# One attention and FFN layer on one core: maxima, reads, loads and digits at other places of a period

## The chip, the cores and the metric

The kernel runs on one core of a Trainium2 chip. The metric is the device time of one execution in microseconds, lower is better. Three runs of the kernel before gave 1106.81, 1106.3 and 1104.47 us, median 1106.3.

## What is computed

The reference is one transformer layer on four sequences (B = 4) of 512 tokens and 1024 features: causal attention with 16 heads of 64 and rotary embedding, a LayerNorm over x plus attention, a linear layer with int8 weights and one scale per output row, and a second LayerNorm.

```python
q, k, v = x @ w_q.T, x @ w_k.T, x @ w_v.T          # split into 16 heads of 64
q, k = rope(q), rope(k)
scores = where(causal, q @ k.T, -1e9) / sqrt(64)
out = softmax(scores) @ v                          # back to (4, 512, 1024)
x = layernorm(x + out @ w_out.T)
x = layernorm(x + x @ (weight * scales[:, None]).T)
```

## The kernel before, in words

All large products run in fp32r, a format with fewer digits than float32. A float32 factor is therefore split into a high part and a low part ("digits"): `high_x` and `high_w` write the high part on ScalarE, `low_x` and `low_w` the low part on VectorE, and `diff_x`, `diff_w` a third tile d, which the product needs beside h and l. `split_w` is `low_w` followed by `diff_w`. `diff_x_apart` is `diff_x` in two instructions on GpSimd. The digits of a sequence's x live in `XD[b % 2]` (two sets), those of the weights of q, k, v in `WD[0..2]`. A product of one unit with one weight is 24 matmuls of 128x512: 16 with the h and l digits, alternating, then 8 with d.

A unit is one sequence and one pair of heads. There are 32 units: sequences 0 and 1 alternate over head pairs 0 to 7, then 2 and 3 alternate over head pairs 7 to 0. The loop over `u` makes one period for each unit. In period u TensorE runs, in this order: `attend(u-1)` (probabilities times values, L528), `scores(u)` (L420) and 72 "tickets" of the stream, which `take(n)` draws: the products k and v of unit u+1 and q of unit u+2 (L273). The last period draws the first four halves of the output projection instead (`out_product`, L200). After the loop come the rest of the output projection and the FFN (L200, L755).

The softmax of a unit goes in three groups g = 2, 1, 0 of the score rows, each in its own PSUM tile. For each group `maxima` takes a minimum with the mask (L444) and the row maxima (L447) on VectorE, `softmax` the exponentials on ScalarE (L461), and `transposes` a 32x32 block transpose on VectorE (L489) and a write to DRAM, `turned<-pr` (L490). `fetch(u, g)` reads it back in its transposed order, `prT<-turned` (L501: one DMA each for g = 2 and 1, two for g = 0). `attend(u)` needs all of them, at the end of the period. `shares` computes the reciprocals of the row sums and writes them (`turned_d`, L475), `fetch_shares` reads them back spread over the partitions (L481); `attended(u-1)` scales with them on GpSimd (L556, L558) and writes the result `ao` (L559). `turn_values` and `fetch_values` do for v what the transposes do for the probabilities (`turned_v`, L490, and `va`, L515).

A finished product is read out of PSUM by ScalarE (L293, after matmul 16) and VectorE (L321, after matmul 24). For q and k `swap` then copies even rows to odd rows and back with two DMAs (L245), and `rope` computes the rotary embedding, for q on GpSimd ("turned_q"), for k on VectorE ("turned_k"). PSUM has two buffers for the products (`pj`).

All DMAs of the loop are issued by SyncE (SP) in program order; an issue that must wait holds what is behind it. ScalarE, VectorE and GpSimd also run in the program's order. Work that must be done in some period, but not at a place that the loop itself names, is put on a plan with `later(u, slot, f)` and done at `run(u, slot)`. The slots stand in the loop in this order: "early", "turned_q", "between", "then", "after", "first", "turn", "mid", "second", "turned_k", "late", "end". Loads of x, of the weights and of `ao` go through three staging buffers (`stage`), which are used in turn; a load waits until the digits of what was there have been made.

Weights of the next head pair are loaded in every odd period that is followed by another head pair (`load_w`, three loads of 512 KB, L182). At four places the digits of x must be replaced: units 14 and 15 are the last of sequences 0 and 1, and units 30 and 31 the last of 2 and 3, after which `XD` receives the two halves of the output weight (L161). `new_sequence(u, b, begin)` does this: with `begin` it issues three loads at the first ticket of product v of unit u, that is in period u-1 inside `take(8)`; without, it makes the high digits and plans the rest. The first tiles of `ao` for the output projection are loaded by `load_ao(k)` (L187) during the products of the last unit, and their digits are put on the plan beside them.

## Time and profile before

The profiled execution took 1109.1 us and its span is 1106.9 us; the median of the runs shown is 1106.3 us. The mean granted TensorE clock is 0.969.

| what | from the profile |
|---|---|
| TensorE busy with matmuls | 1015.2 us, 92% of the span |
| VectorE, ScalarE, GpSimd busy | 774.4, 405.5, 258.8 us |
| DMA | 213.35 MB, mean 193 GB/s |
| the 32 periods and what is ahead of them | up to 824.8 us |
| the rest, output projection and FFN | 282 us |

A period is counted here from the copy of attend's result on ScalarE (L549) to the next one; the starts are read off the timeline of that line. Lengths in us by the period's number:

| period | 1 | 2 | 3 | 4 | 5 | 6 | 7 | 8 | 9 | 10 | 11 | 12 |
|---|---|---|---|---|---|---|---|---|---|---|---|---|
| us | 22.2 | 25.0 | 22.2 | 23.4 | 22.5 | 24.9 | 21.8 | 22.8 | 23.3 | 21.6 | 22.6 | 21.5 |

| period | 13 | 14 | 15 | 16 | 17 | 18 | 19 | 20 | 21 | 22 |
|---|---|---|---|---|---|---|---|---|---|---|
| us | 29.3 | 31.5 | 25.7 | 22.6 | 22.8 | 25.0 | 21.8 | 22.5 | 21.9 | 25.5 |

| period | 23 | 24 | 25 | 26 | 27 | 28 | 29 | 30 | 31 |
|---|---|---|---|---|---|---|---|---|---|
| us | 22.8 | 24.9 | 22.3 | 24.5 | 22.7 | 22.7 | 29.1 | 29.3 | 38.8 |

Period 0 and the start before it end at 65.5 us. In the profile's lines a tile's name stands as out<-in; "p" is a product, "s" the scores and attend's result, "pr" the probabilities, "sx", "sw" and "sa" the staged x, weights and ao, "raw" a product on its way to rope. Line numbers are those of the kernel before.

### The profile page before, as it was taken

The page shows a single profiled execution, that of the slowest core. Times are in us where ns is not written, and L with a number is a line of the kernel's source. Part 1 is how long each engine was busy: PE and PEld are TensorE (multiplying, and loading weights), DVE is VectorE, ACT ScalarE, POOL GpSimd, SP SyncE. Part 2 cuts the span into 40 slices and gives each one's busy share as a digit, 9 for nine tenths or more (in the row PEclk, how much of TensorE's full clock was granted, in tenths as well). Part 3 has the DMA queues.
Part 4 walks back from the last instruction along what each step waited for, and adds up shares of the span by engine and source line. Part 5 has one row for each costly group of instructions (what it writes and reads, how often), then busy time and mean ns, then how long its engine had stood idle before and what let it go on. Part 6 is the DMA issues. An engine that isn't in the chain of part 4 may idle for free.

```text
span 1106.9 us, 17050 instructions
## 1 busy us (share of the span) xinstructions
PE 1015.2 (92%) x6292; PEld 800.3 (72%) x6292; DVE 774.4 (70%) x1104; ACT 405.5 (37%) x873; POOL 258.8 (23%) x206
## 2 busy tenths in 40 slices
PE   9988999899999779899998999997689999999997
PEld 3667777777777657677776777775467888888885
DVE  5776676666767675766757666676678878787766
ACT  4434354343643344253542535434423121212010
POOL 0123342232422544233332334322010000000000
PEclk9989999999999889999999999998989999999999
DMA  7567667687687567676785766777843565656451
GB/s 270 148 190 235 217 195 235 189 251 221 193 257 230 164 217 232 194 221 210 220 256 167 235 205 194 241 227 218 248 141 106 155 156 135 165 126 160 100 129 57
DMA packets 286115, 213.35 MB, mean 193 GB/s; under 512 B 153264, under 2 KB 242352, under 8 KB 285904
## 3 DMA queue, kind: packets, MB, share of 16 engines
q1 hardware_dynamic: 282800, 201.91, 61.5%
q0 software_dynamic: 2224, 8.00, 1.9%
q10 hardware_dynamic: 1008, 2.36, 0.6%
q8 instruction: 50, 0.82, 0.3%
q14 instruction: 33, 0.27, 0.1%
HBM read 120.98 MB, written 74.45 MB: 177 GB/s over the span
## 4 chain that ended last, share of the span: by engine, by line
PE 45%; DMA 20%; DVE 17%; SPq 6%; issue 5%; ACT 5%; POOL 1%; DVEq 0%; ACTq 0%; POOLq 0%
PE y L200 13%; PE p L273 13%; PE f L755 11%; DMA prT<-turned 5%; PE s L528 5%; ACT pr L461 4%; DMA turned_v<-vt 3%; DVE nmx L447 3%; DMA raw<-raw 3%; DMA turned<-pr 2%; PE s L420 2%; DVE pr L489 2%; DVE w_d L224 2%; DVE s L444 2%; DVE raw L321 2%
## 5 line engine op out<-in xcount | busy, mean ns | idle before, releaser
L273 PE MATMUL p<-x_h,w_h 128*128 128x512 f32 x736 | 291.7, 396 | 3.7 <-DVE raw L321 3.7
L273 PE MATMUL p<-x_l,w_l 128*128 128x512 f32 x736 | 288.1, 392 | 0.0
L273 PE MATMUL p<-x_d,w_d 128*128 128x512 f32 x736 | 184.9, 393 | 17.4 <-DVE raw L321 9.4
L273 PEld LDWEIGHTS p<-x_d,w_d 128*128 128x128 f32 x736 | 137.0, 188 | 52.7 <-DVE raw L321 15.3
L461 ACT ACTIVATE pr<-s,nmx 128x512 f32<-128x512 f32 (+3 forms) x256 | 131.7, 526 | 93.0 <-DVE nmx L447 57.9
L273 PEld LDWEIGHTS p<-x_h,w_h 128*128 128x128 f32 x736 | 138.7, 188 | 34.9 <-DVE raw L321 4.5
L273 PEld LDWEIGHTS p<-x_l,w_l 128*128 128x128 f32 x736 | 138.9, 189 | 28.0
L556 POOL TENSOR_TENSOR ot<-ot,ot 128x448 f32<-128x448 f32 x32 | 36.8, 1150 | 436.7 <-ACT ot L550 436.7
L528 PE MATMUL s<-prT,va 64*64 64x64 f32 (+4 forms) x1408 | 96.0, 402 | 45.1 <-DMA prT<-turned 32.4
L489 DVE STREAM_TRANSPOSE pr<-pr 128x768 f32<-128x768 f32 (+1 forms) x96 | 102.1, 1064 | 40.7 <-ACT pr L461 39.0
L528 PEld LDWEIGHTS s<-prT,va 64*64 64x64 f32 x1408 | 72.1, 155 | 74.0 <-issue 60.8
L200 PE MATMUL y<-x_l,w_l 128*128 128x512 f32 x256 | 102.2, 399 | 7.9 <-DVE w_l L220 7.9
L447 DVE TENSOR_REDUCE nmx<-s 128x2 f32<-128x1024 f32 (+3 forms) x128 | 102.1, 820 | 9.1 <-PE s L429 6.1
L293 ACT ACTIVATE raw<-p 128x512 f32<-128x512 f32 x92 | 55.1, 599 | 142.2 <-PE p L273 140.9
L200 PE MATMUL y<-x_h,w_h 128*128 128x512 f32 x256 | 102.4, 400 | 2.4 <-DVE row L209 1.6
L321 DVE SCALAR_TENSOR_TENSOR raw<-p,raw 128x512 f32<-128x512 f32 x92 | 62.6, 680 | 52.9 <-PE p L273 37.1
L755 PE MATMUL f<-wf,x1hi 128*128 128x512 f32 x240 | 94.8, 395 | 2.0 <-ACT x1hi L728 2.0
L755 PE MATMUL f<-wf,x1lo 128*128 128x512 f32 x240 | 94.8, 395 | 0.3 <-DVE x1lo L729 0.3
L444 DVE TENSOR_TENSOR s<-s,bounds 128x256 f32<-128x256 f32 x116 | 48.9, 421 | 61.7 <-PE s L420 60.6
L420 PE MATMUL s<-qk 64*64 64x64 f32 (+5 forms) x1280 | 83.8, 368 | 1.6 <-ACT ot L550 1.6
L420 PEld LDWEIGHTS s<-qk 64*64 64x64 f32 x1280 | 65.6, 137 | 15.6 <-ACT ot L550 11.0
L549 ACT COPY ot<-s 128x512 f32<-128x512 f32 x32 | 18.7, 585 | 156.3 <-PE s L528 156.3
(120 smaller groups left out, 1357.0 us busy)
## 6 DMA issues: line engine op xcount, KB each, us to landing
turned<-pr SPq DMA_DIRECT2D x64, 384.0 KB, 2.7
raw<-raw SPq DMA_DIRECT2D x128, 128.0 KB, 4.1
turned<-pr SPq DMA_DIRECT2D x32, 512.0 KB, 2.9
prT<-turned SPq DMA_DIRECT2D x32, 512.0 KB, 4.3
prT<-turned SPq DMA_DIRECT2D x32, 384.0 KB, 4.2
turned_v<-vt SPq DMA_DIRECT2D x32, 256.0 KB, 4.6
va<-turned_v SPq DMA_DIRECT2D x128, 64.0 KB, 2.7
prT<-turned SPq DMA_DIRECT2D x32, 256.0 KB, 4.8
```

The lines of the kernel that those rows point to most:

```text
L200: nc.tensor.matmul(ps, lhsT=r[part][:, c, :], rhs=w[part][:, c, :], start=n in (0, 2 * NC), stop=n in (2 * NC - 1, NT - 1),)
L273: nc.tensor.matmul(ps, lhsT=w[part][:, c, :], rhs=r[part][:, c, :], start=n in (0, 2 * NC), stop=n in (2 * NC - 1, NT - 1),)
L293: nc.scalar.activation(raw_tile(u, k), ps, AF.Copy, scale=1.0 + X12)
L321: nc.vector.scalar_tensor_tensor(r, ps, -X12, r, op0=MUL, op1=ADD)
L420: nc.tensor.matmul(ps[c * D : (c + 1) * D, j, at + s0 : at + s1], lhsT=t[rows, 0, early : early + D], rhs=t[rows, 1, s0:s1], start=s0 == 0 ...
L444: nc.vector.tensor_tensor(diag, diag, tri, ALU.min)
L447: nc.vector.tensor_reduce(nmx[:, 2 * i : 2 * i + 2], ps[:, :, at : at + n], AX.X, ALU.max, negate=True)
L461: nc.scalar.activation(pr[:, :, at // P : at // P + i + 1, j, :].rearrange("p r k (c s) -> p r k c s", c=2), ps[:, j, at : at + n].rearran ...
L489: nc.vector.transpose(t.rearrange("p (r i s) -> p r i s", r=R, s=16) if by_place else t, by_place or t)
L528: nc.tensor.matmul(ps[j * D : (j + 1) * D, h, at : at + n], lhsT=lhsT, rhs=rhs, start=kb == 0 and at == h * D, stop=kb == NI - 1,)
L556: nc.gpsimd.tensor_tensor(o[:, D:], o[:, D:], o1[:, D:], ADD)
L755: nc.tensor.matmul(ps, lhsT=part[:, c, :], rhs=wfv[:, c, o], start=(c == 0 and part is hi), stop=(c == NC - 1 and part is lo),)
```

## The change

The diff has five parts. First, in the loop: all three `maxima` stand ahead of the transposes, and the three transposes follow each other. Second, on SP: the reads of groups 2 and 1 stand ahead of `take(8)`, in which the swap of k is issued, and the read of group 0 ahead of the write of the shares. "between" moves from ahead of `take(8)` to behind the reads of the shares, with a new slot "loads" behind it. Third, `new_sequence` is planned ahead for all four places: the loads of three staging buffers (two for unit 15) are issued in "early" of period u-1, the high digits are made in "second"; for unit 15 the third load goes to "loads" and its high digit to "end". Fourth, `diff_w(2)` of a new head pair goes from VectorE ("then") to GpSimd, in a new slot "beside" behind the rope of q. Fifth, for the last unit `load_ao(2)` goes to "loads", and the digits of `ao` tile 2 are made at the end of period 30 instead of in periods 30 and 31; `diff_w` of tile 0 follows its `low_w` at once; in period 0 `diff_x(0, 3)` goes from "late" to "between".

```diff
             if more and n == 0 and last:
-                load_ao(k)
+                if k < 2:
+                    load_ao(k)
+                else:
+                    later(u - 1, "loads", lambda: load_ao(2))
...
-            b_next = units[u + 2][0] if u + 2 < NU else B + b % 2
-            x_next = k == 2 and b_next != b
-            if x_next and n == 0:
-                new_sequence(u, b_next, True)
             if n == 2 * NC - 1:
                 nc.scalar.activation(raw_tile(u, k), ps, AF.Copy, scale=1.0 + X12)
-                if x_next:
-                    new_sequence(u, b_next, False)
                 if more and last:
-                    if k < 2:
-                        later(u - 1, ("after", "second")[k], lambda: high_w(k))
-                    else:
-                        high_w(k)
-                    l, d = (("turn", "mid"), ("late", "late"), ("after", "after"))[k]
-                    later(u - (k < 2), l, lambda: low_w(k))
-                    if k == 2:
-
-                        later(u, l, lambda: low_x(b_next, 0))
-                    later(u - (k < 2), d, lambda: diff_w(k))
+                    later(u - 1, ("after", "second", "end")[k], lambda: high_w(k))
+                    later(u - 1, ("turn", "late", "end")[k], lambda: split_w(k))
                 elif more:
...
                         later(u - 1, "end", lambda: low_w(2))
-                        later(u, "then", lambda: diff_w(2))
+                        later(u, "beside", lambda: diff_w(2, nc.gpsimd))
...
-        def new_sequence(u, b, begin):
-            if b == B + 1:
-                if begin:
-                    later(u - 1, "mid", lambda: load_x2(b, 0))
-            else:
-                for n in range(3):
-                    (load_x2 if begin else high_x)(b, n)
-            if begin:
-                return
+        def new_sequence(u, b):
...
+            first = (0, 1, 2) if u % 2 == 0 else (0, 1)
             if b <= B:
-                steps = (
-                    (u - 1, "late", each(low_x, 0)), (u - 1, "late", each(load_x2, 3)),
-                    (u - 1, "late", each(low_x, 1, 2)), (u, "between", each(high_x, 3)),
-                    (u, "between", each(low_x, 3)), (u, "between", each(diff_x, 0, 1)),
-                    (u, "late", each(diff_x, 2, 3)) if b == B else (u, "between", each(diff_x_apart, 2, 3)),
-                )
+                later(u - 1, "early", each(load_x2, *first))
+                later(u - 1, "second", each(high_x, *first))
+                later(u - 1, "late", each(low_x, 0))
+                later(u - 1, "late", each(load_x2, 3))
+                later(u - 1, "late", each(low_x, *first[1:]))
+                if u % 2:
+                    later(u - 1, "loads", each(load_x2, 2))
+                    later(u - 1, "end", each(high_x, 2))
+                    later(u, "between", each(low_x, 2))
+                later(u, "between", each(high_x, 3))
+                later(u, "between", each(low_x, 3))
+                later(u, "between", each(diff_x, 0, 1))
+                if b < B:
+                    later(u, "between", each(diff_x_apart, 2, 3))
+                else:
+                    later(u, "late", each(diff_x, 2, 3))
+                return
...
+        for u in range(1, NU):
+            b_next = units[u + 2][0] if u + 2 < NU else B + units[u][0] % 2
+            if b_next != units[u][0]:
+                new_sequence(u, b_next)
...
-            later(0, "late", lambda: diff_x(0, 3))
+            later(0, "between", lambda: diff_x(0, 3))
...
                 run(u, "turned_q")
+                run(u, "beside")
+                maxima(u, 0)
                 take(18)
-                transposes(u, 2)
-                maxima(u, 0)
                 softmax(u, 0)
-                transposes(u, 1)
-                transposes(u, 0)
+                for g in (2, 1, 0):
+                    transposes(u, g)
                 fetch(u, 2)
-                run(u, "between")
+                fetch(u, 1)
                 run(u, "then")
                 take(8)
+                fetch(u, 0)
                 shares(u)
-                fetch(u, 1)
-                fetch(u, 0)
                 fetch_shares(u)
+                run(u, "between")
+                run(u, "loads")
```

In the built program no instruction is added or dropped; 14 of VectorE's `diff_w` stand on GpSimd.

More of the change, by code (lines that the diff above doesn't have):

```diff
@@ L344, in new_sequence @@
             if b <= B:
-                steps = (
-                    (u - 1, "late", each(low_x, 0)), (u - 1, "late", each(load_x2, 3)),
-                    (u - 1, "late", each(low_x, 1, 2)), (u, "between", each(high_x, 3)),
-                    (u, "between", each(low_x, 3)), (u, "between", each(diff_x, 0, 1)),
-                    (u, "late", each(diff_x, 2, 3)) if b == B else (u, "between", each(diff_x_apart, 2, 3)),
-                )
-            else:
-                steps = (
-                    (u - 1, "late", each(load_x2, 1)), (u - 1, "late", each(high_x, 0)),
-                    (u - 1, "late", lambda: load_x2(b, 2, qkp.tile([P, 2, S], FP, tag="qk", name="last_2"))),
-                    (u, "early", lambda: load_x2(b, 3, qkp.tile([P, 2, S], FP, tag="qk", name="last_3"))),
-                    (u, "then", each(high_x, 1, 2)), (u, "after", each(low_x, 1, 2)),
-                    (u, "first", lambda: more_rows(2)), (u, "first", each(high_x, 3)),
-                    (u, "second", lambda: more_rows(3)), (u, "late", each(low_x, 3)),
-                    (u, "late", each(diff_x, 0, 1, 2, 3)),
-                )
@@ L362, in new_sequence @@
-            for step in steps:
+                later(u - 1, "early", each(load_x2, *first))
[7 more added lines that the diff above has]
+                    later(u, "between", each(low_x, 2))
@@ new lines, in new_sequence @@
+                later(u, "between", each(high_x, 3))
[6 more added lines that the diff above has]
+                return
+            for step in (
+                (u - 1, "mid", each(load_x2, 0)),
+                (u - 1, "late", each(load_x2, 1)), (u - 1, "late", each(high_x, 0)),
+                (u - 1, "late", lambda: load_x2(b, 2, qkp.tile([P, 2, S], FP, tag="qk", name="last_2"))),
+                (u, "early", lambda: load_x2(b, 3, qkp.tile([P, 2, S], FP, tag="qk", name="last_3"))),
+                (u, "then", each(low_x, 0)),
+                (u, "then", each(high_x, 1, 2)), (u, "after", each(low_x, 1, 2)),
+                (u, "first", lambda: more_rows(2)), (u, "first", each(high_x, 3)),
+                (u, "second", lambda: more_rows(3)), (u, "late", each(low_x, 3)),
+                (u, "late", each(diff_x, 0, 1, 2, 3)),
+            ):
```

## The prediction

> **What bounds the kernel now.** I read the page first: TensorE is busy 92% of the span, so an ordinary period cannot become much shorter. The shortest is 21.5 us (period 12). The other 30 together are (785.7 + 38.8 − 65.5) − 21.5 − 30 × 21.5 ≈ 93 us above it, 55 of them in periods 13 to 15 and 29 to 31. The waits say who holds TensorE:
>
> ```profile
> PE s L528 <- DMA prT<-turned: 32.4, 14, 5.3
> PEld p L273 <- DVE raw L321: 19.8, 16, 2.4
> SPq L515 <- DMA turned_v<-vt: 87.6, 19, 6.6
> ```
>
> (Engine, line, releaser: us in total, times, longest.) attend waits for the last prT read, the products wait for VectorE to empty a PSUM buffer, and SP itself waits for turned_v. The chain of waits through periods 13 and 14 (start, us, what) shows the dear places:
>
> ```profile
> 355.78 7.95 DMA prT<-turned
> ...
> 363.86 4.32 PE s L528 x29
> ...
> 380.68 3.12 DVE x_d L178 x2
> 383.80 0.60 DVE raw L321
> ...
> 388.97 6.34 DMA prT<-turned
> ```
>
> The loads of x stand ahead of the prT reads, the last of which lands 7.95 us after its issue (4.1 to 5.2 in periods 17 and 18), and in period 14 VectorE makes x digits before it empties k, so that swap and reads start 5 us late. Attend itself takes 4.3 us here, 2.4 in period 17: the clock has fallen. The same shows in stretches of period 18 (length, busy us of TensorE, its weight loads, VectorE, ScalarE, GpSimd, granted clock, DMA share, GB/s):
>
> ```profile
> 491.00:493.00 2.00, 0.98 (x9) 0.77 (x13) 2.00 (x3) 0.00 (x0) 0.00 (x0) 0.69 0.59 206
> 493.00:495.00 2.00, 2.00 (x22) 1.29 (x17) 1.93 (x2) 0.00 (x0) 0.00 (x0) 0.50 0.22 74
> ```
>
> A gap of 2.5 us costs the gap and some 2 us of half clock: even periods with gaps of 2.3 to 2.8 us last 24.5 to 25.5 us (period 4 alone 23.4), those with 1.6 to 1.8 us 22.5 to 22.8. Last, VectorE in odd period 17, which sets the product's wait:
>
> ```profile
> 452.97 1.25 DVE L489 STREAM_TRANSPOSE pr<-pr 128x1024 f32<-128x1024 f32 x1 [0.23 <-ACT pr L461]
> 454.14 0.87 DVE L444 TENSOR_TENSOR s<-s,bounds 128x256 f32<-128x256 f32 x2
> 455.04 1.02 DVE L447 TENSOR_REDUCE nmx<-s 128x2 f32<-128x256 f32 x2
> 455.98 0.97 DVE L489 STREAM_TRANSPOSE pr<-pr 128x768 f32<-128x768 f32 x1
> 457.85 0.98 DVE L489 STREAM_TRANSPOSE pr<-pr 128x768 f32<-128x768 f32 x1 [0.90 <-ACT pr L461]
> 458.75 1.18 DVE L224 TENSOR_TENSOR w_d<-w_h,w_l 128x1024 fp32r<-128x1024 f32 x1
> 459.86 0.68 DVE L321 SCALAR_TENSOR_TENSOR raw<-p,raw 128x512 f32<-128x512 f32 x1
> ```
>
> **Odd ordinary periods (12).** With the maxima ahead, group 0's are done at 452.7 + 0.87 + 1.02 ≈ 454.7 instead of 456.1; its exponentials (1.73 us) start behind the ScalarE read that ends at 454.7. The last transpose then ends at about 457.9 instead of 458.8, and without w_d (1.18) L321 ends at 458.6 instead of 460.5. The product's gap there (0.5 to 1.1 us, 1.13 in period 17) goes, and the last read is issued 1 us earlier. Against it: group 2's transpose is 1.7 us later, its write too; this is covered, since its read waited on SP until 459.3 for the third write's issue. The swap of k now waits behind the group 1 read, 384 KB or 1.5 us of a full queue (249 GB/s at 439 to 441 us), so k lands about 1 us later. Behind k on VectorE are turn_values and, in even periods, w_l (1.18), L321 of q (0.68), w_d (1.21) and w_l (1.22): they ended at 449.81, and period 17's first minimum started only then. So after an undisturbed even period the whole of this lateness, up to 1.6 us, passes to the odd period and eats its gain; after an even period with a lost clock there is room. Gain 1.1 us in about half, 0 to −0.3 in the rest: −0.4 each, −4.8. Bounds: −1.3 and +0.8 each.
>
> w_d takes 2.41 us on GpSimd (its row in period 16) and starts after the rope of q, at 456.1, so it ends at 458.5; the matmuls that read it start at 459.1 (40 matmuls of 0.225 us from 450.1). Cover 0.7 us; without it, TensorE waits for the difference. Beside GpSimd's two-step digits x_l takes 1.87 and 2.19 us (1.23 alone), but in period 16 L321 (0.69 at 438.80) ran unslowed beside this same w_d (438.19 to 440.60): I take 0; were each L321 slowed like x_l, 14 × 0.5 = 7 us. The Trainium skill, "SBUF — State Buffer", section "Who interferes with whom", says that a VectorE instruction with two SBUF inputs and a GpSimd one that reads SBUF lock each other out for the whole instruction. By it, VectorE's neighbours here (transposes with one input, L321 with one from PSUM) would not be touched, and the sum stays; a lock on all two-input instructions would make it up to 14 × 1.2 = 17 us worse.
>
> **Even ordinary periods (13).** The queue is full from the writes to attend (DMA share 0.9 to 1.07 between 481 and 489 us), so the order of reads matters little: only turned_d's 16 KB leave the path, about −0.3. But turned_d now lands behind the last read, some 2 to 2.5 us later, and SP holds the shares' reads, the three weight loads and turned_v behind it. In odd periods this moves 1.75 MB back; the loads' queue took 8.5 us to turned_v's landing, some of it at 102 GB/s, so part is made good. SP waits for that landing in the next even period before va, ao and the writes (5.4 us in period 18). I take +0.5 − 0.3 = +0.2 each, +2.6. Bounds: −0.8 (loads make it all good), +1.3 (all of it passes on).
>
> **The first replacement of x (13 to 15).** Period 13: the loads (1.5 MB, 3.9 us at 394 GB/s) move ahead of va, where the queue idles (0.2 to 0.5 DMA share at 449 to 453 in period 17), 5 us before the writes need it. va has 15 us of cover. The gap of 5.05 us goes and the half clock behind it: from 29.3 to an ordinary 22.2, −7. Period 14: L321 of k no longer waits for x_l and x_d (1.87 + 3.12), −5 of gap, −3 of clock, −1.7 at the products' x_h. A new wait: ScalarE makes the high digit of the third load at "end", ahead of the copy of attend's result; this load is issued on SP behind the shares, at about 20.4 us of the period, and lands some 4 to 5 us later (row<-in_x, the same size with little ahead of it: 3.9; sx: 5.8); its digit costs 1.06: the copy starts at about 26.5 instead of 22, and TensorE stands at the scores. Period 14 takes 26.5, −5. Period 15: without L321's late start −2.5, but x_d on GpSimd (1.88 + 3.23) ends late for the last products and the clock may fall: 24.2, −1.5. Sum −13.5; bounds −20 (all three at 22) and −7 (both new waits double).
>
> **The second (29 to 31).** Period 29 like 13: −7. Period 30 ends today in a chain that the change lengthens (start, us, what):
>
> ```profile
> 779.11 5.87 DMA sx<-in_wo
> ...
> 785.96 0.57 ACT ot L549
> ...
> 806.68 5.83 DMA row<-in_x
> ```
>
> Ahead of that load stands load_ao(2) now (512 KB, 1.3 us), and behind its digit ScalarE makes w_h and its scaled copy (1.04 + 1.06) before attend's copy; shorter gaps earlier in the period give back 2.6: +0.8. In period 31 the wait of 7.5 us for w_l (L200) goes, but the end hangs on row<-in_x, issued behind the shares, and these 1.0 us later behind turned_d; x_l and x_d follow on VectorE. +1.1. Sum −5.1; bounds −14 (the 7.5 us count, period 30 gains 1) and +1.
>
> **Period 0:** x_d's gap of 5.95 us goes, but the last prT read lands 0.6 us before that gap's end: −0.6, bounds −0.8 and +0.5.
>
> **Sum:** −4.8 + 2.6 − 13.5 − 5.1 − 0.6 = −21.4 us. The profiled span 1106.9 (execution 1109.1, 2.8 above the median) becomes 1085.5; from the median 1106.3: 1084.9, so 1085.
>
> On the clock: the Trainium skill, "TensorE: Matmul & The Clock Gate", section "What's actually happening", puts the fall after an idle window of about 3.4 us, so gaps of 2.5 us would cost nothing beyond themselves. Here they do, by the rows above (clock 0.69 and 0.50). By the page, six even periods would lie no lower and the slow rival below would be some 10 us cheaper.
>
> **Rivals.** (1) *Slower:* turned_d behind the last read. If all of its 2 to 2.5 us reaches turned_v, even periods start their writes 1.3 us later, the six with short gaps lose the clock as well (1.7 each), and the odd ones inherit VectorE's lateness (+0.8): 13 × 1.3 + 6 × 1.7 + 12 × 0.8 = +36.7, less 19.2 from the replacements and period 0, +17.5: 1124. It decides from 19.2 / 25 = 0.77 us lost per ordinary period. For it: turned_v already is SP's longest wait, 87.6 us. Against: the queue has slack at 467 to 469 us (share 0.71). 0.13. (2) *Better:* all odd periods gain 1.1, all even ones 0.3, and both new waits of ScalarE are covered (4.5 in period 14, 1.9 in 30 and 31): −13.2 − 3.9 − 18.6 − 6.4 − 0.6 = −42.7: 1064. For it: the waits named first do go; against: the full queue. 0.14. (3) *The loads come no earlier:* a staging buffer is free only after w_l at the period's begin (until 340.5 in period 13), then loads, va and the first write meet, and most of the gap reappears: replacements gain 5, ordinary periods 0: 1101. For it: the third buffer is the last one freed; against: the first write is needed 7 us later. 0.13. The forecast has 0.60.
>
> **How the numbers follow.** The measurement tells from no change what exceeds 0.2%, 2.2 us. The groups' low ends add up to −60.8, the high ends to +21.0; half the way from the sum to each gives 1065 to 1106, since they will not all fall on one side. That holds the forecast, rival 3 and half of 2, and leaves out rival 1: range 1065 to 1106. Faster: the forecast but for 0.02, rival 2 and 0.08 of rival 3: 0.80. Same: those 0.02 and 0.04 of rival 3: 0.06. Slower: rival 1 and the last 0.01 of 3: 0.14.
>
> **What would show it.** Right: prT reads of periods 13, 14, 29 land 4 to 5 us after issue; no L321 wait in odd periods; a wait of ScalarE's x_h on sx at the ends of periods 14 and 30. Wrong: even periods at 25 us throughout, SP's wait at L515 (now va) above 100 us, or VectorE's first minimum later than 2 us in odd periods. If period 13 stays above 24 us, the loads did not move.

## The result, and the profile after

The changed kernel takes 1143.4 us (median of 4 runs, 1140.1 to 1148.6), the kernel before beside it 1106.6 us: a ratio of 1.0334, 95% interval 1.0284 to 1.0384. The profiled execution took 1145.4 us, its span is 1143.6 us against 1106.9, its mean granted clock 0.950 against 0.969. The forecast was 1085 us, the range 1065 to 1106.

Where the 36.7 us of span went, in us, by the lengths of the periods (measured as in the table of before, from copy to copy on ScalarE; an ordinary period is one outside 0, 13 to 15 and 29 to 31):

| | before | after | difference | forecast |
|---|---|---|---|---|
| 12 odd ordinary periods | 268.8 | 267.9 | −0.9 | −4.8 |
| 13 even ordinary periods | 306.9 | 351.4 | **+44.5** | +2.6 |
| periods 13, 14, 15 | 29.3, 31.5, 25.7 | 22.3, 29.1, 25.9 | −9.2 | −13.5 |
| period 29 | 29.1 | 23.1 | −6.0 | −7 |
| period 30 | 29.3 | 40.3 | **+11.0** | +0.8 |
| period 31 | 38.8 | 39.5 | +0.7 | +1.1 |
| period 0 and the start | 65.5 | 64.5 | −1.0 | −0.6 |
| all behind the periods | 282.2 | 279.8 | −2.4 | 0 |

Two lines hold the whole loss. First the waits of TensorE and VectorE after (engine, line, releaser: us in total, times, longest); L523 is attend, L310 the read of a product's PSUM buffer, L237 the rope's first step:

```profile
DVE raw L237 <- DMA raw<-raw: 170.5, 31, 9.1
...
PE s L523 <- DMA prT<-turned: 70.8, 22, 5.9
...
PEld p L273 <- DVE raw L310: 3.8, 2, 1.9
```

The wait for VectorE is all but gone (it was 19.8), as forecast, but attend waits 70.8 us for the prT reads instead of 32.4, and VectorE 170.5 us for the swap of k instead of 72.1. SP's own waits say what they hang on (L476: the shares' reads, L510: va):

```profile
SPq L476 <- DMA turned_d<-rdenT: 128.4, 32, 5.5
SPq L510 <- DMA turned_v<-vt: 91.9, 28, 7.1
```

The first was 44.0 before:

```profile
SPq L481 <- DMA turned_d<-rdenT: 44.0, 30, 4.0
```

SP's issues around the begin of even period 8 (start, us, what) show how one wait becomes the other. Before, where the period begins at 227.5 us:

```profile
218.69 0.54 SPq L475 DMA_DIRECT2D turned_d<-rdenT  x1
219.33 1.50 SPq L501 DMA_DIRECT2D prT<-turned  x3
221.22 1.31 SPq L481 DMA_DIRECT2D share<-turned_d  x2
222.58 0.60 SPq L182 DMA_DIRECT2D sw<-in_wq  x1
...
224.23 0.59 SPq L490 DMA_DIRECT2D turned_v<-vt  x1
...
232.44 1.91 SPq L515 DMA_DIRECT2D va<-turned_v  x3
```

After, where it begins at 233.1 us:

```profile
224.47 1.29 SPq L496 DMA_DIRECT2D prT<-turned  x2
225.81 0.58 SPq L470 DMA_DIRECT2D turned_d<-rdenT  x1
230.59 1.31 SPq L476 DMA_DIRECT2D share<-turned_d  x2
231.95 0.60 SPq L182 DMA_DIRECT2D sw<-in_wq  x1
...
233.60 0.56 SPq L485 DMA_DIRECT2D turned_v<-vt  x1
```

And the chain of waits through the same stretch, after:

```profile
225.81 4.76 DMA turned_d<-rdenT
...
233.60 8.11 DMA turned_v<-vt
...
245.59 3.76 DMA turned<-pr
...
251.69 5.21 DMA prT<-turned
256.90 0.14 issue
257.03 4.32 PE s L523 x29
```

turned_d is 16 KB, yet it lands 4.76 us after its issue, just behind the last prT read. SP stands until then; the three weight loads and turned_v, which program order puts behind, are issued only from 231.95 on; turned_v stands behind 1.5 MB of weights and lands 8.6 us into the even period (233.60 + 8.11); only then does SP issue va (8.6 us into the period, 5.0 before), ao and the writes of this period's probabilities. Attend starts at 257.0, and TensorE has lost its clock meanwhile (length, busy us of TensorE, its weight loads, VectorE, ScalarE, GpSimd, granted clock, DMA share, GB/s):

```profile
253.00:255.00 2.00, 0.00 (x0) 0.00 (x0) 0.00 (x0) 0.00 (x0) 0.00 (x0) 1.00 1.12 309
255.00:257.00 2.00, 0.00 (x0) 0.00 (x0) 1.29 (x2) 0.00 (x0) 0.00 (x0) 0.64 0.18 41
257.00:259.00 2.00, 1.97 (x19) 1.14 (x22) 1.99 (x3) 0.00 (x0) 0.00 (x0) 0.50 0.05 16
```

Before, this period lasted 22.8 us with a gap of 1.8 us and full clock; now 28.5 with 5.2 and half clock. Over the 13 even periods the gaps ahead of attend grew from 25.2 to 55.7 us. The other 14 of the 44.5 us are slower work behind the gaps, most of it attend itself: it takes 52.4 us in these periods instead of 41.2, and over 3 us in 11 of the 13 instead of 6.

VectorE in odd period 17, beside the lines of before:

```profile
465.51 0.89 DVE L439 TENSOR_TENSOR s<-s,bounds 128x256 f32<-128x256 f32 x2
466.43 1.02 DVE L442 TENSOR_REDUCE nmx<-s 128x2 f32<-128x256 f32 x2
467.37 2.95 DVE L484 STREAM_TRANSPOSE pr<-pr 128x1024 f32<-128x1024 f32 x3
470.25 0.65 DVE L310 SCALAR_TENSOR_TENSOR raw<-p,raw 128x512 f32<-128x512 f32 x1
```

Maxima, three transposes, k's buffer: the order is the one wanted. It begins late here, because VectorE was still behind from the even period. On the mean of the odd ordinary periods L310 of k ends 10.2 us into the period (11.9 before), but the first minimum starts at 1.7 (1.0) and k's swap lands at 18.0 (15.8).

Last, the replacements. ScalarE's waits for the late loads, periods 14 and 30:

```profile
ACT x_h L165 <- DMA sx<-in_wo: 20.9, 1, 20.9
...
ACT x_h L165 <- DMA sx<-in_xT: 10.5, 1, 10.5
```

and the chain through the end of period 30 and into 31:

```profile
810.09 11.19 DMA sx<-in_wo
...
821.30 1.06 ACT x_h L165
822.36 0.95 ACT w_h L215
...
824.30 0.57 ACT ot L544
...
846.62 5.74 DMA row<-in_x
```

The load of 512 KB takes 11.2 us, with two loads of 512 KB from ScalarE's queue (the tables' rows) and ao's third tile issued 0.8 to 2.2 us ahead of it; two digits follow, and attend's copy comes 40.3 us into the period. In period 31 the wait for w_l is 3.3 us instead of 7.5, but TensorE waits 13.6 us for the row load behind the shares: the predicted exchange.

### The profile page after: what moved, and what is told of

Read it like the earlier page. It is cut to its first block, busy times and chain, and to the rows that moved or that the text cites. A ratio compares the mean times of both kernels' runs of the same rounds, so it can differ in the third digit from the quotient of the medians.

```text
span 1143.6 us, 17116 instructions
## 1 busy us (share of the span) xinstructions
PE 1022.3 (89%) x6292; PEld 807.8 (71%) x6292; DVE 766.5 (67%) x1090; ACT 401.1 (35%) x873; POOL 309.3 (27%) x220
## 4 chain that ended last, share of the span: by engine, by line
PE 42%; DMA 32%; SPq 9%; DVE 9%; issue 4%; ACT 3%; POOL 1%; DVEq 0%; ACTq 0%; POOLq 0%
PE y L200 13%; PE f L751 10%; PE p L273 9%; DMA turned<-pr 8%; DMA prT<-turned 7%; DMA turned_v<-vt 7%; PE s L523 6%; DMA turned_d<-rdenT 4%; PE s L415 3%; DMA raw<-raw 2%; SPq L245 2%; DVE pr L484 2%; SPq L496 2%; SPq L510 2%; ACT pr L456 1%
## 5 line engine op out<-in xcount | busy, mean ns | idle before, releaser
L523 PE MATMUL s<-prT,va 64*64 64x64 f32 (+4 forms) x1408 | 105.7, 434 | 72.0 <-DMA prT<-turned 70.8
L273 PEld LDWEIGHTS p<-x_d,w_d 128*128 128x128 f32 x736 | 137.5, 188 | 37.5 <-DVE raw L310 3.8
L523 PEld LDWEIGHTS s<-prT,va 64*64 64x64 f32 x1408 | 76.2, 166 | 105.7 <-issue 61.7
L551 POOL TENSOR_TENSOR ot<-ot,ot 128x448 f32<-128x448 f32 x32 | 39.4, 1231 | 411.7 <-ACT ot L545 399.0
L237 DVE TENSOR_TENSOR raw<-raw,sin_sb 128x512 f32<-128x512 f32 x33 | 23.4, 708 | 170.5 <-DMA raw<-raw 170.5
L200 PE MATMUL y<-x_h,w_h 128*128 128x512 f32 x256 | 102.6, 401 | 13.6 <-DVE row L209 13.6
L484 DVE STREAM_TRANSPOSE pr<-pr 128x768 f32<-128x768 f32 (+1 forms) x96 | 97.8, 1046 | 11.9 <-ACT pr L456 11.6
L310 DVE SCALAR_TENSOR_TENSOR raw<-p,raw 128x512 f32<-128x512 f32 x92 | 61.6, 670 | 59.5 <-PE p L273 59.3
L415 PE MATMUL s<-qk 64*64 64x64 f32 (+5 forms) x1280 | 86.9, 380 | 12.6 <-ACT ot L545 12.6
L415 PEld LDWEIGHTS s<-qk 64*64 64x64 f32 x1280 | 69.6, 143 | 25.5 <-ACT ot L545 21.3
```

The source lines that it names most:

```text
L200: nc.tensor.matmul(ps, lhsT=r[part][:, c, :], rhs=w[part][:, c, :], start=n in (0, 2 * NC), stop=n in (2 * NC - 1, NT - 1),)
L237: engine.tensor_tensor(rot, rot, sin_sb[:, k, :], MUL)
L273: nc.tensor.matmul(ps, lhsT=w[part][:, c, :], rhs=r[part][:, c, :], start=n in (0, 2 * NC), stop=n in (2 * NC - 1, NT - 1),)
L310: nc.vector.scalar_tensor_tensor(r, ps, -X12, r, op0=MUL, op1=ADD)
L415: nc.tensor.matmul(ps[c * D : (c + 1) * D, j, at + s0 : at + s1], lhsT=t[rows, 0, early : early + D], rhs=t[rows, 1, s0:s1], start=s0 == 0 ...
L484: nc.vector.transpose(t.rearrange("p (r i s) -> p r i s", r=R, s=16) if by_place else t, by_place or t)
```

## The experiments

All lengths below are us by class of period from each kernel's own profile; the time is the median, with the ratio to the kernel before on the same chip (its medians there: 1100.8 to 1102.7). "d" is the place of the shares' write turned_d on SP, "k" that of k's swap.

| kernel | odd | even | 13–15 | 29 | 30 | 31 | time | ratio (95%) |
|---|---|---|---|---|---|---|---|---|
| before | 268.8 | 306.9 | 86.5 | 29.1 | 29.3 | 38.8 | 1106.6 | |
| after | 267.9 | 351.4 | 77.2 | 23.1 | 40.3 | 39.5 | 1143.4 | 1.033 (1.028–1.038) |
| e1 | 258.5 | 340.3 | 77.1 | 21.7 | 37.6 | 39.7 | 1122.0 | 1.019 (1.014–1.024) |
| e2 | 258.1 | 307.8 | 73.2 | 22.2 | 34.9 | 37.7 | 1080.9 | 0.980 (0.975–0.986) |
| e3 | 266.3 | 353.6 | 85.0 | 25.9 | 37.9 | 41.3 | 1160.5 | 1.053 (1.048–1.058) |
| e4 | 260.3 | 353.2 | 79.9 | 22.8 | 35.2 | 39.0 | 1133.5 | 1.030 (1.025–1.036) |
| e5 | 269.7 | 301.4 | 72.7 | 23.8 | 32.1 | 34.9 | 1079.9 | 0.981 (0.978–0.984) |
| e6 | 254.7 | 347.5 | 78.8 | 22.5 | 37.0 | 39.9 | 1125.8 | 1.022 (1.019–1.025) |
| e7 | 255.8 | 303.7 | 73.1 | 22.4 | 28.8 | 37.5 | 1072.5 | 0.975 (0.971–0.979) |
| e8 | 252.6 | 280.1 | 71.2 | 21.3 | 31.0 | 37.0 | 1040.5 | 0.945 (0.942–0.948) |
| e9 | 259.5 | 297.7 | 85.0 | 28.2 | 28.3 | 35.5 | 1088.9 | 0.989 (0.985–0.993) |
| e10 | 263.4 | 312.4 | 86.0 | 27.2 | 28.8 | 36.9 | 1104.3 | 1.003 (1.000–1.006) |
| e11 | 268.4 | 308.0 | 71.9 | 22.5 | 28.6 | 38.6 | 1083.8 | 0.986 (0.983–0.990) |
| e12 | 275.7 | 300.6 | 80.1 | 21.6 | 38.0 | 40.2 | 1107.2 | 1.006 (1.004–1.009) |
| e13 | 256.4 | 293.2 | 80.2 | 22.6 | 36.1 | 38.5 | 1076.7 | 0.978 (0.974–0.982) |
| e14 | 275.2 | 281.7 | 72.3 | 24.0 | 31.2 | 34.9 | 1065.7 | 0.969 (0.965–0.973) |
| e15 | 266.7 | 279.0 | 87.1 | 27.8 | 28.5 | 37.8 | 1074.8 | 0.975 (0.972–0.979) |
| e16 | 257.2 | 278.1 | 72.2 | 23.3 | 28.5 | 36.5 | 1042.1 | 0.946 (0.943–0.950) |

The lengths are of one execution of each kernel. How far two executions differ can be seen where the programs are the same up to period 29: the odd and even periods together are 565.9 us in e2 and 559.5 in e7, 619.2 in the changed kernel and 613.5 in e4. Differences of 6 us, or of 8 in one class, therefore show nothing by themselves.

### The order of SP's reads: e1, e2, e3

e1 is the changed kernel with the write of the shares ahead of the last read:

```diff
                 take(8)
-                fetch(u, 0)
                 shares(u)
+                fetch(u, 0)
                 fetch_shares(u)
```

> The changed kernel with one step put back: the write of the shares (turned_d) and the two steps before it on VectorE stand ahead of the read of group 0 again; the read of group 1 stays ahead of the swap of k. Theory A (turned_d lands behind the last prT read and holds back the shares' reads, the weight loads, turned_v and so the writes of the next even period): the even ordinary periods fall from 27.0 us on the mean to 23.6 or less, their sum from 351 to about 307, SP's wait for turned_d from 128 to about 45 us in all, and the total to about 1143 - 44 = 1099 us (1090 to 1108). Rival B (k's swap behind the read of group 1 is what makes the even periods late): nothing of this, the evens stay at 26 to 27 us and the total above 1130. Rival C (the digit on GpSimd or the maxima): the same as B.

e2 puts back the whole order of reads:

```diff
                 fetch(u, 2)
-                fetch(u, 1)
                 run(u, "then")
                 take(8)
-                fetch(u, 0)
                 shares(u)
+                fetch(u, 1)
+                fetch(u, 0)
```

> The changed kernel with the whole order of SP's reads as before: only group 2 ahead of the eighth products and the swap of k, then the write of the shares, then groups 1 and 0. Theory A: as with the write of the shares alone put back, within some 5 us (1093 to 1105): the read of group 1 has no large part. Rival B: only this one falls, to 1100 or less, and the kernel with the write alone put back does not. Rival C: even periods stay at 26 to 27 us, the total above 1130.

e3 is the kernel before with this one part of the change (the same diff the other way, "between" where it was):

> The kernel before with only the order of SP's reads changed: groups 2 and 1 ahead of the eighth products, group 0 ahead of the write of the shares. Theory A: the even ordinary periods grow by about 3 us each, the total is about 1106 + 44 = 1150 us (1140 to 1165, since the odd periods have no gain to set against it here). Rival C (digit on GpSimd, maxima): the total stays at 1104 to 1110.

The order of reads is the whole loss of the ordinary periods: without it (e2) the changed kernel is 20 us faster than before, alone (e3) it costs 59 us. But e1 missed: one read less ahead of turned_d took only 11 us off the evens, not 44. By its profile turned_d still lands 17.6 us into the odd periods (15.8 in e2, 19.5 after), turned_v 6.9 us into the even ones (5.2, 7.9). That only e2 falls below 1100 us is what rival B had said, and e2 is faster than theory A allowed. Theory A could still stand in a wider form, that any read ahead of turned_d delays it. e1 differs from e2 in both: the read of group 1 stands ahead of turned_d and ahead of k's swap. Hence the next two.

### The write of the shares or the swap of k: e5, e6

e5: d right behind the read of group 2, k behind the read of group 1.

```diff
                 fetch(u, 2)
+                shares(u)
                 fetch(u, 1)
                 run(u, "then")
                 take(8)
                 fetch(u, 0)
-                shares(u)
```

> The changed kernel with the shares' write (turned_d) right behind the read of group 2, ahead of the read of group 1, which stays ahead of the swap of k. Theory A, by now in the form that whatever read stands ahead of turned_d's write on SP's queue delays it, and with it turned_v and the even periods (write behind one read: 26.2 us per even period, behind two: 27.0, behind group 2's alone: 23.7): turned_d lands at about 12 to 15 us of the odd periods, the evens fall to about 23.7 us, the total to 1080 to 1092 us (before 1101 to 1107). Rival B (the swap of k behind the read of group 1 sets the evens): the evens stay near 26 us, the total near 1120.

e6: k ahead, d still last.

```diff
                 fetch(u, 2)
-                fetch(u, 1)
                 run(u, "then")
                 take(8)
+                fetch(u, 1)
                 fetch(u, 0)
                 shares(u)
```

> The changed kernel with the swap of k ahead of the read of group 1 as before, but the shares' write (turned_d) still last, behind the reads of groups 1 and 0. Theory A: the evens stay at 26 to 27.5 us, the total at 1125 to 1150. Rival B: the evens fall to 23.7 us and the total to 1080 to 1095 us.

Theory A holds at both: e5 at 1079.9, e6 at 1125.8, with 23.2 and 26.7 us to the even period. SP's waits in e6, beside the changed kernel's 128.4 and 91.9:

```profile
SPq L476 <- DMA turned_d<-rdenT: 130.4, 32, 5.5
SPq L510 <- DMA turned_v<-vt: 106.4, 28, 7.3
```

The swap of k is not free: e5's odd periods are 11.6 us longer than e2's, since k lands 1.2 us later in the even ones and VectorE's first minimum in the odd ones starts at 2.2 instead of 1.2 us. Its even periods are 6.4 us shorter, so that its time is e2's.

### The weight loads between the shares and turned_v: e8, e12, e15, and e13, e14

One edit: SP issues the loads of a new head pair behind the write of turned_v.

```diff
                 run(u, "loads")
-                if u % 2 and u + 2 < NU - 1 and units[u + 2][1] != units[u + 3][1]:
-                    for k in range(3):
-                        load_w(k, units[u + 3][1])
...
                 if u + 1 < NU:
                     turn_values(u + 1)
+                if u % 2 and u + 2 < NU - 1 and units[u + 2][1] != units[u + 3][1]:
+                    for k in range(3):
+                        load_w(k, units[u + 3][1])
```

e8 has it on top of e7 (below), e12 on the changed kernel, e15 on the kernel before.

> The kernel with the old order of reads and the old last unit, and with the three weight loads of a new head pair (1.5 MB) moved on SP from behind the shares' reads to behind the write of turned_v. Theory A's last link (turned_v lands some 8 us after its issue because the weight loads stand ahead of it, and SP holds the even period's va reads and writes until then): turned_v lands 2 to 5 us after its issue in odd periods, SP's wait for it in even periods goes from about 5 us to under 1, their first write of probabilities from about 9 to about 7 us, and the 13 even periods fall from 23.7 to about 22 us: some 20 us less than its neighbour, about 1057 us. Rival F (the even periods are set by the bytes in the queue, not by when turned_v lands: the loads only move into the next period and delay its reads as much): the time stays within 5 us of the neighbour's.

> The changed kernel, its order of reads and all, with only the three weight loads of a new head pair moved from behind the shares' reads to behind the write of turned_v. Theory A's last link (the late write of the shares costs the even periods only because turned_v stands behind 1.5 MB of weights): turned_v lands about 3 us after its issue, 2 us or less into the even periods, these fall from 27.0 to 22 or 23 us, and the total to 1075 to 1095 us: the place of the shares' write costs next to nothing here. Rival I (the lateness of k's swap and of the shares themselves is enough): the total stays above 1115.

> The kernel before with one edit that the change does not have: the three weight loads of a new head pair behind the write of turned_v. Theory A (turned_v behind the weight loads sets the even periods whatever the rest does): the even periods fall from 307 to about 284 us, the odd ones from 269 to about 266, the total by 24 to 30 us, ratio about 0.975. Rival (it pays only together with the earlier maxima and loads): less than 10 us.

SP's issues in e8 around the begin of even period 8 (213.5 us):

```profile
204.45 0.56 SPq L472 DMA_DIRECT2D turned_d<-rdenT  x1
205.09 1.60 SPq L498 DMA_DIRECT2D prT<-turned  x3
208.20 1.32 SPq L478 DMA_DIRECT2D share<-turned_d  x2
210.68 0.34 SPq L487 DMA_DIRECT2D turned_v<-vt  x1
211.07 0.43 SPq L182 DMA_DIRECT2D sw<-in_wq  x1
...
214.34 3.45 SPq L512 DMA_DIRECT2D va<-turned_v  x4
```

va is issued 0.8 us into the period instead of 8.6 in the changed kernel; SP's wait for turned_v is 7.2 us in the whole run. The evens fall to 280 us, e8 to **0.945 of the time before**, the fastest of all: 32 us below e7, where theory A said 20. e15 shows that this needs nothing of the change: 26 us from the kernel before alone. e12 fell between its two theories: it takes back 43 us of odd and even periods, but 43.6 more than e8 remain, so the order of reads still costs something. e13 is e12 with k ahead (e6 and this edit), e14 with d ahead (e5 and this edit).

> The swap of k ahead of the read of group 1 as before, the write of the shares still behind the last read, the weight loads behind turned_v's write. Beside the changed kernel with the weight loads moved alone (1107 us, odd and even ordinary periods together 576 us) this differs by the place of k's swap. Theory K (what remained there is k's swap: VectorE begins its odd periods 2.7 us late): odd and even together fall to 533 to 545 us, the total to 1060 to 1075. Theory S (the shares' write still holds turned_v): they stay above 565 us, the total above 1090.

> The mirror of it: the write of the shares right behind the read of group 2, the swap of k behind the read of group 1, the weight loads behind turned_v's write. With the loads at their old place this took 1080 us, odd and even ordinary periods together 571. Theory K: these stay at 560 us or more, the total at 1065 to 1080. Theory S: they fall to 533 to 545 us, the total to 1040 to 1055.

Neither theory alone. Odd and even ordinary periods together:

| | loads ahead of turned_v | loads behind it |
|---|---|---|
| old order | 565.9 (e2) | 532.7 (e8) |
| k behind the read of group 1 | 571.0 (e5) | 556.9 (e14) |
| d behind the last read | 602.2 (e6) | 549.6 (e13) |
| both, as in the change | 619.2 (after) | 576.3 (e12) |

With the loads in the way d costs 36 us and k 5 (no more than two executions differ by), together 53; with the loads out of the way 17 and 24, together 44. What is left of d's price goes the same way: turned_v lands 2.4 us into the even periods of e13 and 0.7 us ahead of them in e8, and their first write is issued at 8.5 instead of 7.2 us. The late k costs the odd periods: VectorE around the end of even period 6 in e14 (197.4 us):

```profile
193.13 0.69 DVE L237 TENSOR_TENSOR raw<-raw,sin_sb 128x512 f32<-128x512 f32 x1 [4.38 <-DMA raw<-raw]
...
196.80 0.68 DVE L310 SCALAR_TENSOR_TENSOR raw<-p,raw 128x512 f32<-128x512 f32 x1
197.40 1.21 DVE L224 TENSOR_TENSOR w_d<-w_h,w_l 128x1024 fp32r<-128x1024 f32 x1
198.53 2.19 DVE L220 SCALAR_TENSOR_TENSOR w_l<-w_h,sw 128x1024 fp32r<-128x1024 f32 x1
```

VectorE waits 4.38 us for the swap, and what stands behind runs 3.3 us into the odd period; on the mean the first minimum starts at 2.8 us there, at 0.9 in e8.

### One part alone: e9, e10, e11, e16

e9 is the kernel before with the first part of the change (maxima ahead, transposes together), e10 with the fourth (v's third digit to GpSimd), e11 with the third (the loads of a new sequence). e16 is e8 with v's third digit back on VectorE.

```diff
-                take(18)
-                transposes(u, 2)
                 maxima(u, 0)
+                take(18)
                 softmax(u, 0)
-                transposes(u, 1)
-                transposes(u, 0)
+                for g in (2, 1, 0):
+                    transposes(u, g)
```

> The kernel before with one part alone: group 0's maxima ahead of the 18 products, the three transposes together behind its exponentials. Theory G (this part and the third digit on GpSimd share the gain of the odd periods, by how much earlier each lets VectorE empty k's buffer: 0.9 of 2.1 us): the 12 odd periods lose 4 to 5 us of their 269, the even ones nothing, the ratio is about 0.996. Theory H (the product's gap of 0.5 to 1.1 us is closed by either part alone): 8 to 10 us, ratio about 0.992. Rival: group 2's write, 1.7 us later, costs as much: ratio 1.000 or more.

```diff
-                        later(u, "then", lambda: diff_w(2))
+                        later(u, "beside", lambda: diff_w(2, nc.gpsimd))
...
                 run(u, "turned_q")
+                run(u, "beside")
```

> The kernel before with one part alone: the third digit of v's weights made by GpSimd behind the rope of q instead of by VectorE ahead of its read of k's buffer. Theory G: 5 to 7 us in the odd periods, ratio about 0.994. Theory H: 8 to 10 us, ratio about 0.992. Rival (GpSimd slows VectorE beside it, 7 to 17 us by the bounds of the prediction): ratio 1.000 or more, and the VectorE reads of PSUM beside the digit take over 0.69 us.

> The kernel before with one part alone: the loads of a new sequence at the begin of a period and their digits at their new places (the third digit of period 0 and the slot of the late digits with them); maxima, order of reads, v's third digit and the last unit as before. If the gain of the replacements comes from this part alone: periods 13 to 15 together fall from 86.5 to about 74 us, period 29 from 29.1 to about 22.5, the ordinary periods stay (odd 269, even 307), the total falls by 18 to 22 us, ratio about 0.982. Rival (they gain only because k's buffer is emptied earlier by the other parts): less than half of that.

e16, the fourth part undone in e8:

```diff
-                        later(u, "beside", lambda: diff_w(2, nc.gpsimd))
+                        later(u, "then", lambda: diff_w(2))
```

> The fastest version so far (old order of reads, old last unit, weight loads behind turned_v; 1040.5 us) with v's third digit back on VectorE ahead of its read of k's buffer. If the digit on GpSimd pays once turned_v no longer sets the pair of periods: the odd periods grow by 0.5 to 1.1 us each, the total to 1047 to 1053 us. If it pays nothing (alone in the kernel before it made 1.0028 of the time): within 3 us of 1040.5.

e9's ratio of 0.989 (0.985 to 0.993) fits theory H; in its profile the odd periods gain 9.3 us and the even ones, which no theory had named, 9.1. e10 closes the same gap (TensorE's wait for L321 falls from 19.8 to 4.3 us in both) and gains nothing in its time, against both theories. The rival's number came true (1.003), but not its reason: no VectorE read of PSUM beside GpSimd took over 0.69 us. In its profile the odd periods are 5.4 us shorter and the even ones 5.5 longer, differences that show nothing by themselves; SP's wait for turned_v is not shorter:

```profile
SPq L515 <- DMA turned_v<-vt: 93.1, 18, 7.2
```

(87.6 before.) The difference is what reaches SP. On the mean of the odd periods the maxima let group 0's write go 1.0 us earlier and the first read 0.6, turned_d lands at 15.5 instead of 16.1 us and turned_v is issued at 18.5 instead of 19.2. With the digit the first read is where it was (10.7, before 10.6); turned_d is issued 0.7 us earlier and yet lands at 16.5, and turned_v is issued at 19.6. So nothing that SP stops for comes earlier; why turned_d takes longer to land there was not tried. In e16 VectorE makes the digit again, and the time is e8's within its uncertainty: TensorE's wait for VectorE's read is 1.9 us in both, since the maxima close the gap by themselves (e9). e11 gives the replacements what was forecast for them: 13 to 15 lose 14.6 us, 29 loses 6.6, the ordinary periods nothing.

### The end of the units: e4, e7

The weights of the last unit as before, on the changed kernel (e4) and on e2 (e7):

```diff
-                if k < 2:
-                    load_ao(k)
-                else:
-                    later(u - 1, "loads", lambda: load_ao(2))
+                load_ao(k)
...
-                    later(u - 1, ("after", "second", "end")[k], lambda: high_w(k))
-                    later(u - 1, ("turn", "late", "end")[k], lambda: split_w(k))
+                    if k < 2:
+                        later(u - 1, ("after", "second")[k], lambda: high_w(k))
+                    else:
+                        high_w(k)
+                    l, d = (("turn", "mid"), ("late", "late"), ("after", "after"))[k]
+                    later(u - (k < 2), l, lambda: low_w(k))
+                    later(u - (k < 2), d, lambda: diff_w(k))
```

> The changed kernel with the weights of the last unit and the first output column as before: the third load of the attention's result at the third product's begin, its high digit and its scaled copy at that product's end, its low and third digits in the last period. Theory D (ScalarE's digit of this late load in period 30 holds its copy of attend's result, and the load is late because it stands behind the shares and the tables): period 30 falls from 40.3 to about 33 us (29.3 before, and 3.4 more for an even period with the late write of the shares), period 31 keeps 39 to 41, the total is about 1136 us. Rival E (period 30 is long because of the loads of wo alone, whatever the weights do): period 30 stays at 38 us or more and the total at 1141 or more.

> The changed kernel with the whole order of SP's reads as before, and the weights of the last unit and the first output column as before. With the order alone put back it took 1080.9 us (before 1101.3 beside it), its period 30 34.9 us and period 31 37.7. Theory D (ScalarE's digit of the late load holds the copy of attend's result): period 30 falls to about 30 us, period 31 rises to about 39, the total is some 4 us lower, about 1077. Rival E (the loads of wo alone make period 30 long): period 30 stays above 34 us, the total does not fall.

Period 30 falls by 5.1 us in e4 and by 6.1 in e7, period 31 by 0.5 and 0.3: theory D, smaller in e4 than expected (35.2 instead of 33). ScalarE's wait for wo is 6.6 us in e4 and 3.3 in e7 instead of 20.9 and 16.7. The other half of period 30's loss is the order of reads again: 40.3 to 34.9 us from the changed kernel to e2.

## Why the prediction was wrong

**Even ordinary periods: the step that failed.** "The queue is full from the writes to attend, so the order of reads matters little", and then "I take +0.5 − 0.3 = +0.2 each", with +1.3 as the bound where all of it passes on. Measured: +3.4 each. I had the right chain (turned_d, the shares, the loads, turned_v, va, the writes) and priced it as bytes in a queue, where it is a series of stops in SP's program: what is late at a stop is late at each that follows, and the slack that I saw in the queue made good little of it. Term by term: turned_d lands 3.4 us later in the odd periods (19.5 instead of 16.1), not 2 to 2.5; the even periods' va is issued 2.8 us later (7.9 instead of 5.1), not 0.5; their first write 2.65 us later (11.2 instead of 8.55); and the gap that this opens, 4.2 to 5.4 us in most of them, costs the clock too, which the bound of +1.3 left out, although the forecast itself had read that price off period 18. Rival 1 named the mechanism, with "1.3 us later" per even period in place of 2.65; it gave 1124. Of the signs of being wrong, the even periods came true (27.0 us on the mean, the sign was 25); SP's wait for turned_v stayed at 91.9 us, under its mark of 100, since SP loses the time one stop earlier, at turned_d; the first minimum, at 1.7 us on the mean, stayed under its mark of 2.

**Odd ordinary periods.** "No L321 wait" was right, 19.8 us to 3.8. That k's lateness would eat the gain was right too, but it was taken as 1 us: k lands 2.2 us later in the odd periods and 4.2 in the even ones. With the old order the odd periods gain 10.7 us (e2), 0.9 each, near the 1.1 taken for an undisturbed one. But the digit added nothing to the time: alone it closed the gap and nothing came of it (e10), and beside the maxima there was nothing left to close (e16).

**The replacements.** Right in mechanism and nearly in size: period 13 at 22.3 (forecast 22.2), 29 at 23.1 (22.2), and e11 alone −14.6 for 13 to 15 (−13.5). In the changed kernel 14 is an even period with late writes, and ScalarE's wait for the third load is 10.5 us: 29.1, not 26.5. e2 has 24.7 there.

**Period 30.** "+0.8" was mis-sized: the wait of x_h on sx was foreseen, its 11.2 us of landing were not. I had taken the load at 5.87 us and one tile of ao ahead of it, and left out the two loads of 512 KB from ScalarE's queue: before, they start 1.6 us behind the load of wo, now 2.2 and 1.9 us ahead of it. In e7, where they again start behind it and no ao stands ahead, it lands in 5.85 us. No run moves the tables alone, so how much is theirs and how much ao's stays open. Half of the +11.0 is this placement (5 to 6 us by e4 and e7), half the late reads.

**GpSimd's digit.** It took 2.41 us and slowed nothing: 14 of VectorE's L310 ran beside it in e2, at 0.65 us each (0.68 alone). The cover held too: in the changed kernel TensorE's weight loads waited 3.2 us in all for a w_d of GpSimd, but in five even periods and for the one that stood there before. The price of 0 stands.

With the order of reads put back, e2 is 20.4 us faster than the kernel before beside it, and the forecast said 21.4 for the whole. That the two are so near is in part luck: in e2 the odd periods gain 10.7 us instead of the 4.8 forecast, and period 30 loses 5.6 instead of 0.8. In rival 2, 18.6 and 6.4 should read 18.0 and 7.0 by its own terms; its sum stands.

## What to carry to other kernels

Read an in-order DMA-issuing engine as a program with stops: list the instructions at which it waits for a landing, and price a moved transfer by what stands ahead of it on the queue when it is issued, then carry the delay through every later stop, nearly one to one (3.4 us became 2.8 here). A small transfer that a stop hangs on belongs ahead of large ones, and large ones that nobody waits for belong behind the one that the next stop needs: moving three loads behind one write was worth 26 us alone, and 32 on top of e7, where it gave the fastest kernel, 5.5% faster than before. And closing a wait on one engine can gain nothing while another engine's stops come no earlier (the digit alone, e10): ask which of the two moves.

## What the runs showed of the hardware

A write of 16 KB (turned_d) issued last on SP's queue landed 0.15 to 0.21 us behind the last prT read (128 to 512 KB each) in every ordinary period of the changed kernel and of e6; issued ahead of the last three reads, as before and in e2, it landed at least 2.3 us ahead of the last of them. The Trainium skill, "DMA: Bandwidth & Descriptors", section "Queues, rings and completion order", says that the semaphore's increment lands only after every earlier write of that DMA engine; the rows agree, but they don't tell whether the write itself or its increment came late.

VectorE's w_l (L220, two inputs from SBUF) takes 1.22 us alone. In the kernel before one of 58 took over 1.3 us (1.38); in the changed kernel 12 did, 1.58 to 2.33 us, some 9 us more in all. Each of them ran beside a GpSimd instruction, 10 beside the rope of q and 2 beside the work on attend's result. This does not need a late VectorE: the fastest kernel, e8, has 12 as well, all beside the rope, 7.8 us more in all. Where VectorE is late, as in e14, nine more stand beside attend's result, among them the 2.19 us above, whose neighbours on GpSimd are these (same columns):

```profile
198.50 1.14 POOL L551 TENSOR_TENSOR ot<-ot,ot 128x448 f32<-128x448 f32 x1 [8.73 <-ACT ot L545]
199.72 2.15 POOL L553 TENSOR_TENSOR ot<-ot,share 128x512 f32<-128x512 f32 x1
```

L553 itself takes 1.38 us on the mean of the changed kernel. w_l starts 0.03 us behind L551 and ends 1.1 us behind its end, and L553 ends 1.15 us behind w_l's end, as if each had run only when the other was done. That fits the lock of the Trainium skill, "SBUF — State Buffer", section "Who interferes with whom", that the prediction weighed for the digit on GpSimd: it came at another pair, one with two SBUF inputs on VectorE, as the page has it. The page says of such a pair that it contends, and of VectorE's 2-port modes that the lock holds for the whole instruction; these rows look like the latter. That the lock is the reason is the page's word; no run here tries another.

Half clock followed gaps of attend of 2.04 us (period 17 of the changed kernel: 0.50 at 482 to 484 us) and 1.83 us (period 23: 0.50 at 632 to 634), but not one of 2.02 us (period 18: 1.00 at 505 to 509), nor one of 2.33 us in period 4 of the kernel before (1.00 at 155 to 159). So the length of a gap alone doesn't tell whether the clock falls; what else decides was not tried.
